# First-unit inputs in one queue, the mask spread by a product, both first units ahead of the scores: a cross-attention and feed-forward kernel on one core

## The chip, the core and the metric

The kernel runs on one core of a Trainium2 chip. The metric is device time in microseconds (us) of one execution; lower is better. Three timed runs of the kernel before gave 1829.25, 1832.85 and 1832.66 us, median 1832.66. One more execution was profiled, and all durations below come from it. In its views the engines are PE (TensorE matmuls; PEld its weight loads), DVE (VectorE), ACT (ScalarE), POOL (GpSimd) and SP (SyncE, which here only issues DMAs). SPq, ACTq and POOLq are the instruction streams that issue DMAs.

## The reference

Sixteen sequences, each with 256 rows (channels) of 512 positions, float32:

```python
x = x + xattn(layernorm(x), ctx, mask, mask, Wq, bq, Wk, bk, Wv, bv)   # 16 heads of 16 channels
x = x + ffn(layernorm(x), lut, gate_idx, up_idx, down_idx)             # weights are lut[idx], 1376 wide

# xattn: q = Wq @ target + bq, k and v likewise from source; per head
dot = mask * (q.T @ k) / 4 - (1 - mask) * 1e6
out = (softmax(dot) * mask) @ v
```

The layernorm runs over the 512 positions of a row, without weights. The mask is one row of 512 numbers per sequence, used for queries and for keys.

## The kernel before

All of it is float32. The attention part takes the first 1000 us or so, the feed-forward part the rest. This case concerns the first 50 us.

**Units and steps.** Heads are handled four at a time. A *unit* is four heads of one sequence, and there are 64 units. Each head owns a strip of 32 partitions in the tiles `kp` (keys) and `qp` (queries): 16 rows of data and two rows that carry the mask term and the row maximum, so that one 32-row product gives masked scores less their maximum. Each unit has four *steps*, one per 128 query positions. A step makes scores twice. First `pa` (L483) gives the scores that DVE reduces to row maxima (`nm`, L499). Seven steps later `pb` (L491) gives the transposed scores, which ACT turns into exponentials (L503) for the product with the values (L525). Steps are numbered by their `pb`, so steps -7 to -1 have `pa` only, and step 0 is the first with both. The maxima of a unit are turned (`turn_max`, tile `pmx`), copied by DVE and sent by a POOL DMA into `qp`.

**The order is written out by hand.** `scores(sa, sb)` makes the score products of a step. The dictionary `lumps[s]` holds PE work put after the scores of step `s` and `after[s]` what follows it: projections of later units (`project(k, "k")`, `project(k, "q")`), values (`project_v`), sends through DRAM (`send`, `fetch`), statistics (`stats1`), the layernorm of the next sequence (`norm1`, on POOL), and so on. Every engine then runs its own list strictly in this order, and an instruction that has to wait holds up all behind it on that engine. The PSUM pool `ps_a` has two buffers of two banks (the two halves of a `pa`); `ps_b` has four of one bank, shared by everything else on PE.

**Ahead of step -7** come the first units, 0 and 1 (`e` = 0 and 1 of the first eight heads). They do not go through DRAM. `pad(i, e)` copies the wanted columns of `wk` or `wq` into strips of a zeroed tile `w0`; `first_tile(which, e)` multiplies them with the source `cx0` or the normalized rows `xn0`, adds a per-row column `bcol` and multiplies with a mask tile (`mbk` for keys, `mb0` for queries). `bcol` is a transpose (tile `pbrow`) of the small tile `brow`, into which four POOL DMAs bring biases. `mbk` is the mask row broadcast to 128 partitions by a DMA, two rows of each strip then being overwritten by two more DMAs (L376, L377): the mask less one, computed by DVE at L375 from `mk16`, and ones. `mb0` is the plain broadcast. `row_stats` (L100, L101), `rstd1_of` (ACT's square root at L105, then L106 and L107) and `norm1` (L282) normalize `xn0`. `warm(n)` issues n transposes of the identity that nothing reads. Unit 0 is made ahead of step -7; unit 1's `pad` and `first_tile` stand in steps -7 to -4.

**DMA counters.** A DMA that SP or ACT issues signals its landing on one of eight counters, taken in turn. A DMA that takes a counter again first waits, on its own issuing engine, until the counter's earlier DMA has landed.

Of the kernel before, what the change touches and what calls it, by code (L numbers as in the profile page):

```python
# [9 lines left out]
F32 = mybir.dt.float32  # L10
I32 = mybir.dt.int32
AF = mybir.ActivationFunctionType
ALU = mybir.AluOpType
# [6 lines left out]
def kernel(  # L20
# [70 lines left out]
    lut_b = cpool.tile([P, LUT], F32, tag="lut", name="lut_b")  # L91
# [6 lines left out]
    def row_stats(pool, mv, xt, name):  # L98
        st = pool.tile([P, 6], F32, tag="bn", name=f"bn_{name}")
        nc.vector.bn_stats(st, xt)  # L100
        nc.vector.bn_aggr(mv, st)  # L101
# [117 lines left out]
    with ExitStack() as att:  # L219
        ac = att.enter_context(tc.tile_pool(name="att_const", bufs=1))  # L220
        p1 = att.enter_context(tc.tile_pool(name="att1", bufs=1))
        p2 = att.enter_context(tc.tile_pool(name="att2", bufs=2))
        pp = att.enter_context(tc.tile_pool(name="att_p", bufs=3))
        lp = att.enter_context(tc.tile_pool(name="lookup", bufs=1))

        wq = ac.tile([P, NCC, C], F32, tag="wq", name="wq")
# [22 lines left out]
        def times(row, n):  # L249
            return row.rearrange("p (o t) -> p o t", o=1).to_broadcast([1, n, T])  # L250
# [27 lines left out]
        def norm1(b, eng):  # L278
            xn = inp[b][1]
            for o in range(NCC):  # L280
                i = b * NCC + o
                eng.tensor_scalar(  # L282
                    xn[:, o, :], xn[:, o, :], rstd1[:, i : i + 1], nmr1[:, i : i + 1],
                    ALU.mult, ALU.add,
                )

        def set_ones(i):
            nc.gpsimd.memset(vas[i][:, :, :, D : 2 * D], 1.0)
# [3 lines left out]
        xn0 = p2.tile([P, NCC, T], F32, tag="xn", name="xn_0")  # L292
        mb0 = p2.tile([P, T], F32, tag="mb", name="mb_0")
        inp[0] = (cx0, xn0, mb0)
        for o in range(NCC):
            nc.sync.dma_start(xn0[:, o, :], x[0, o * P : (o + 1) * P, :])
        nc.scalar.dma_start(wk, wkT.rearrange("(o p) n -> p o n", p=P))
        nc.scalar.dma_start(cx0, src[0].rearrange("(o p) t -> p o t", p=P))
        nc.sync.dma_start(mk16, mask[:, 0, :])
        nc.sync.dma_start(mb0, mask[0, 0].partition_broadcast(P))  # L300

        w0 = pp.tile([P, 4, NCC, P], F32, tag="pt", name="w0")
        nc.gpsimd.memset(w0, 0.0)
        nc.gpsimd.memset(ones, 1.0)


        brow = pp.tile([P, P], F32, tag="pt", name="brow")
        nc.vector.memset(brow, 0.0)
        nc.vector.memset(brow[0:64, 16:P:32], NEG / QK)
        for i in range(2):  # L310
            nc.vector.memset(brow[64:P, 16 + i : P : 32], 1.0)

        mbk = pp.tile([P, T], F32, tag="pt", name="mbk")
        nc.sync.dma_start(mbk, mask[0, 0].partition_broadcast(P))
        nc.sync.dma_start(wq, wqT.rearrange("(o p) n -> p o n", p=P))
        for i, w in enumerate((bq, bk)):
            for e in range(2):
                at = 64 * i + 32 * e
                nc.gpsimd.dma_start(
                    brow[at : at + 1].rearrange("o (j e d) -> o j e d", e=2, d=D)[:, :, 0],  # L320
                    w[0:P].rearrange("(o j e d) -> o j e d", o=1, e=2, d=D)[:, :, e],
                )
        n = B * NCH
# [5 lines left out]
        nc.scalar.dma_start(wv, wvT.rearrange("(o p) n -> p o n", p=P))  # L329
        nc.scalar.dma_start(bvb, bv.partition_broadcast(P))  # L330
        nc.scalar.dma_start(lut_b, lut.partition_broadcast(P))
        zeros = rpool.tile([P, T], F32, tag="rb", name="zeros", bufs=1)
        nc.gpsimd.memset(zeros, 0.0)

# [13 lines left out]
        def pad(i, e):  # L348
            w = (wk, wq)[i]
            to = w0[:, 2 * i + e].rearrange("p o (j r) -> p o j r", r=32)[:, :, :, 0:16]  # L350
            of = w[:, :, 0:P].rearrange("p o (j e d) -> p o j e d", e=2, d=D)[:, :, :, e]
            if i == 0:
                nc.vector.tensor_copy(to, of)
            else:
                nc.vector.tensor_scalar(to, of, QK, None, ALU.mult)

        def first_tile(which, e):

            i, to, m = (0, kps[e], mbk) if which == "k" else (1, qps[e], mb0)
            ps = ps_b.tile([P, 512], F32, tag="b", name=f"p{which}_first{e}")  # L360
            for o in range(NCC):
                nc.tensor.matmul(
                    ps, w0[:, 2 * i + e, o, :], inp[0][i][:, o, :],
                    start=(o == 0), stop=(o == NCC - 1),
                )
            at = 64 * (1 - i) + 32 * e
            nc.vector.scalar_tensor_tensor(to, ps, bcol[:, at : at + 1], m, ALU.add, ALU.mult)

        def warm(n):
            for _ in range(n):  # L370
                ps = ps_b.tile([P, 512], F32, tag="b", name="warm")
                nc.tensor.transpose(ps[:, :P], ident, ident)

        warm(60)
        nc.vector.tensor_scalar(mk16, mk16, -1.0, None, ALU.add)  # L375
        nc.sync.dma_start(mbk[16:P:32, :], times(mk16[0:1], 4))  # L376
        nc.sync.dma_start(mbk[17:P:32, :], ones[0:4])  # L377
        for o in range(NCC):
            row_stats(p2, mv1[:, o, :], xn0[:, o, :], f"a0_{o}")
        pad(0, 0)  # L380
        rstd1_of(0, 1)
        norm1(0, nc.vector)
        pad(1, 0)
        pc = ps_b.tile([P, 512], F32, tag="b", name="pbrow")
        nc.tensor.transpose(pc[:, :P], brow, ident)
        bcol = pp.tile([P, P], F32, tag="pt", name="bcol")
        nc.vector.tensor_copy(bcol[:, 64:P], pc[:, 64:P])
        nc.vector.tensor_scalar(bcol[:, 0:64], pc[:, 0:64], QK, None, ALU.mult)
        first_tile("k", 0)
        first_tile("q", 0)  # L390
# [23 lines left out]
        def project(k, which):  # L414
            b, oc = divmod(k, NCC)
            cx, xn, mb = inp[b]
            w, src_t = (wk, cx) if which == "k" else (wq, xn)
            ps = ps_b.tile([P, 512], F32, tag="b", name=f"p{which}_{k}")
            in_columns(ps, lambda o, at: w[:, o, at], oc * P, lambda o: src_t[:, o, :])
            t = p1.tile([P, T], F32, tag=f"nat{which}", name=f"nat{which}_{k}")  # L420
            if which == "k":
                nc.scalar.activation(t, ps, AF.Identity, bias=bkc[:, oc : oc + 1])  # L422
            else:
                nc.scalar.activation(t, ps, AF.Identity, bias=bqc[:, oc : oc + 1], scale=QK)
            nc.gpsimd.tensor_tensor(t, t, mb, ALU.mult)  # L425
            nat[which, k] = t
# [14 lines left out]
        def project_v(k, i):  # L441

            b, half = divmod(k, 2)
            cx = inp[b][0]
            c = 2 * half + i
            ps = ps_b.tile([P, 512], F32, tag="b", name=f"pv_{b}_{c}")
            in_columns(ps[:, :C], lambda o, at: cx[:, o, at], c * P, lambda o: wv[:, o, :])
            vt = p2.tile([P, C], F32, tag="vt", name=f"vt_{b}_{c}")
            nc.scalar.copy(vt, ps[:, :C])
            nc.gpsimd.tensor_tensor(  # L450
                vas[b % 2][:, c, :, 0:D], vt.rearrange("p (h d) -> p h d", d=D),
                bvb.rearrange("p (h d) -> p h d", d=D), ALU.add,
            )
# [148 lines left out]
        for k in range(1, NK):  # L602
            t = 8 * k
# [593 lines left out]
```

## Time and profile before

| | |
|---|---|
| median of the timed runs (3) | 1832.66 us (1829.25 to 1832.85) |
| profiled execution, its own time | 1828.26 us |
| its span, first to last instruction | 1826.5 us |
| PE busy over the span | 1800.2 us (99%) |
| DVE busy | 1453.9 us (80%) |
| ACT busy | 800.8 us (44%) |
| PE busy from 0 to 14 us, 14 to 20 us, 20 to 50 us | 12.01, 4.15, 27.41 us |
| start of step -7 (first `pa`), of step 0, of step 2 | 16.67, 40.94, 49.79 us |

The timeline view lists merged instructions with start, duration, engine, line, operation, output, input and count; a square bracket gives the idle time of the engine before it and what ended that. The windows view gives, for stretches of the span, each engine's busy time and instruction count, the clock granted to TensorE (1.00 is full) and what the DMA engines moved. The waits view gives who waited for whom: total us, times, longest.

### The profile page before, as it was taken

Reading aid. Unit: us, or ns where it says so; the run is one execution under the profiler, and the core shown is the slowest. Engines: PE = TensorE matmul, PEld = TensorE weight load, DVE = VectorE, ACT = ScalarE, POOL = GpSimd, SP = SyncE. Lnnn points to the kernel's source line nnn. Section 1 sums busy time; section 2 is a strip of 40 time slices with the busy share of each in tenths; the row PEclk is TensorE's granted clock in tenths of the full one; section 3 lists DMA queues with packets and bytes.
Section 4 is the critical chain, followed back from the end, with each engine's and each line's share of the span. In section 5 each row is a group of like instructions: output and inputs, shape, how many; then the busy total and the mean of one; then the engine's idle time right before and its main releaser. Section 6 shows DMA issues by size and latency. Waiting matters only on the chain.

```text
span 1826.5 us, 28462 instructions
## 1 busy us (share of the span) xinstructions
PE 1800.2 (99%) x10914; PEld 811.5 (44%) x10914; DVE 1453.9 (80%) x1979; ACT 800.8 (44%) x1523; POOL 499.1 (27%) x465
## 2 busy tenths in 40 slices
PE   8999999999999999999999999999999999999999
PEld 4333333333333333333343444444444444588888
DVE  6898999999999999999874699998989964354352
ACT  1777677777777777777777111112121111000000
POOL 4334333434343434343322122222222222000000
PEclk9999999999999999999999999999999999999999
DMA  6545244334443444445242211223121311533531
GB/s 188 152 140 157 90 128 119 118 96 119 130 120 93 116 136 123 128 126 149 91 128 83 75 51 63 75 86 104 64 98 53 110 46 42 183 131 120 182 131 58
DMA packets 118535, 201.07 MB, mean 110 GB/s; under 512 B 21748, under 2 KB 23416, under 8 KB 118400
## 3 DMA queue, kind: packets, MB, share of 16 engines
q1 hardware_dynamic: 114128, 196.21, 34.4%
q0 software_dynamic: 3168, 1.86, 0.5%
q8 instruction: 86, 1.41, 0.3%
q10 hardware_dynamic: 1104, 1.19, 0.2%
q14 instruction: 49, 0.40, 0.1%
HBM read 135.83 MB, written 58.10 MB: 106 GB/s over the span
## 4 chain that ended last, share of the span: by engine, by line
PE 83%; DMA 6%; DVE 5%; issue 2%; SPq 2%; POOL 2%; ACT 0%; POOLq 0%; DVEq 0%; ACTq 0%
PE p L894 27%; PE pa L483 13%; PE q L1100 11%; PE pv L525 10%; PE pb L491 9%; PE pk L409 3%; PE pv L409 3%; PE pq L409 2%; DVE nm L499 2%; PE po L1081 2%; DMA qp<-qd 2%; PE q L1105 1%; PE pgu L874 1%; PE pmx L508 1%; PE pt L215 1%
## 5 line engine op out<-in xcount | busy, mean ns | idle before, releaser
L499 DVE TENSOR_REDUCE nm<-pa 128x2 f32<-128x1024 f32 x512 | 602.0, 1217 | 75.6 <-PE pb L491 70.1
L503 ACT ACTIVATE pt<-pb 128x512 f32<-128x512 f32 x1024 | 531.3, 603 | 114.2 <-PE pb L491 112.5
L483 PE MATMUL pa<-kp,qp 32*128 32x512 f32 x2048 | 520.7, 618 | 12.3 <-DVE nm L499 7.4
L491 PE MATMUL pb<-qp,kp 32*128 32x512 f32 x2048 | 518.8, 619 | 0.0
L483 PEld LDWEIGHTS pa<-kp,qp 32*128 32x128 f32 x2048 | 181.1, 184 | 226.2 <-DVE nm L499 190.4
L525 PE MATMUL pv<-pt,va 128*32 128x512 f32 x2048 | 246.5, 599 | 0.0
L491 PEld LDWEIGHTS pb<-qp,kp 32*128 32x128 f32 x2048 | 201.1, 183 | 74.7 <-issue 46.7
L894 PE MATMUL p<-xe,wu 128*128 128x512 f32 (+1 forms) x336 | 158.1, 593 | 1.0 <-DVE w L898 1.0
L894 PE MATMUL p<-xT,sw 128*128 128x512 f32 (+1 forms) x336 | 157.9, 592 | 0.0
L894 PE MATMUL p<-xT,wg 128*128 128x512 f32 (+1 forms) x336 | 157.9, 592 | 0.0
L921 POOL TENSOR_TENSOR ha<-ha,sg 128x512 f32<-128x512 f32 (+1 forms) x42 | 59.8, 1424 | 345.0 <-DVE ha L898 333.9
L926 ACT ACTIVATE w<-w 128x512 f32<-128x512 f32 (+1 forms) x42 | 26.5, 630 | 239.9 <-DVE w L898 239.9
L525 PEld LDWEIGHTS pv<-pt,va 128*32 128x32 f32 x2048 | 53.4, 109 | 174.1 <-ACT pt L503 97.8
L511 POOL DMA_DIRECT2D qp<-mx x64 | 37.5, 585 | 314.6 <-DVE mx L510 213.1
L1116 ACT COPY q<-q 128x256 f32<-128x256 f32 x14 | 5.2, 372 | 254.1 <-PE q L1100 254.1
L530 ACT COPY us<-pv 128x512 f32<-128x512 f32 x128 | 74.9, 585 | 93.0 <-PE pv L525 92.3
L894 PEld LDWEIGHTS p<-xe,wu 128*128 128x128 f32 (+1 forms) x336 | 62.8, 187 | 83.0 <-issue 72.0
L894 PEld LDWEIGHTS p<-xT,wg 128*128 128x128 f32 (+1 forms) x336 | 62.7, 187 | 79.2 <-issue 76.4
L894 PEld LDWEIGHTS p<-xT,sw 128*128 128x128 f32 (+1 forms) x336 | 62.1, 187 | 75.4 <-issue 73.4
L908 ACT ACTIVATE sg<-sg 128x512 f32<-128x512 f32 (+1 forms) x42 | 26.5, 630 | 154.7 <-DVE sg L898 154.7
L537 POOL TENSOR_TENSOR us<-us,us 128x512 f32<-128x512 f32 x64 | 82.2, 1285 | 16.5 <-ACT us L530 16.4
L425 POOL TENSOR_TENSOR natk<-natk,mb 128x512 f32<-128x512 f32 x31 | 42.8, 1381 | 158.0 <-ACT natk L422 152.4
(182 smaller groups left out, 2373.3 us busy)
## 6 DMA issues: line engine op xcount, KB each, us to landing
x2t<-x SPq DMA_DIRECT2D x96, 256.0 KB
h<-h SPq DMA_DIRECT2D x7, 2560.0 KB
kp<-kd SPq DMA_DIRECT2D x62, 256.0 KB
qp<-qd SPq DMA_DIRECT2D x62, 256.0 KB
h<-ha SPq DMA_DIRECT2D x38, 256.0 KB
h<-hb SPq DMA_DIRECT2D x38, 256.0 KB
rb<-rd SPq DMA_DIRECT2D x32, 256.0 KB
xr<-in_x_dram SPq DMA_DIRECT2D x32, 256.0 KB
```

The lines of the kernel that those rows point to most:

```text
L409: nc.tensor.matmul(ps[32 * j : 32 * j + 32], weights(o, slice(first + 32 * j, first + 32 * j + 32)), moving(o), start=(o == 0), stop=(o == ...
L425: nc.gpsimd.tensor_tensor(t, t, mb, ALU.mult)
L483: nc.tensor.matmul(pa[:, jj, :], qps[ua % 4][at, ca * P : (ca + 1) * P], kps[ua % 4][at, :], start=True, stop=True,)
L491: nc.tensor.matmul(pb, kps[ub % 4][at, cb * P : (cb + 1) * P], qps[ub % 4][at, :], start=True, stop=True,)
L499: nc.vector.tensor_reduce(nms[ua][:, 2 * half : 2 * half + 2, ca], pa, AX.X, ALU.max, negate=True)
L503: nc.scalar.activation(pts[sb][:, j, :], pb, AF.Exp)
L525: nc.tensor.matmul(ps[32 * j : 32 * j + 32, :], va[:, at : at + 32], pt[:, j, :], start=(i == 0), stop=(i == 1),)
L530: nc.scalar.copy(us[u, half], ps)
L537: nc.gpsimd.tensor_tensor(a, a, b, ALU.add)
L894: nc.tensor.matmul(ps, a[:, h, at], b[:, h, :], start=h == 0, stop=h == 1)
L921: nc.gpsimd.tensor_tensor(ha, ha, sg, ALU.mult)
L1100: nc.tensor.matmul(ps, a[:, o, first_t], b[:, o, :], start=o == 0, stop=o == HO - 1 and not more,)
```

## The change

It touches only what stands ahead of step 0.

- **Loads.** `xn0`, `wk`, `cx0`, `wq`, `mk16`, `wv`, `bvb`, `lut_b` are all issued by SP, in this order. The four bias DMAs into `brow` move from POOL to ACT. The three broadcasts and the two patches that made `mbk` and `mb0` are gone.
- **Mask.** Two rows of a zeroed tile `msrc` are loaded with the mask by two ACT DMAs, DVE subtracts one from the second, and two matmuls with a selection tile `sel` (built by DVE memsets) write `mbk` and `mb0` into one PSUM tile `pm`. ACT copies them out.
- **Order.** `warm(60)` becomes `warm(24)` and, after the mask and `bcol`, `warm(12)`. The statistics of `xn0` now follow `bcol`. All four `pad` come next (those with `e` = 1 on ACT) and then all four `first_tile`, ahead of step -7.
- **Steps -7 to 0.** The four lumps that made unit 1 fall away. `project_v` of the first sequence moves from steps -3 to -1 to steps -5 and -4; `project(2, "k")` and `project(2, "q")` move one step earlier, to -2 and -1; `set_ones(1)` moves from step -4 to -6.

```diff
-        nc.scalar.dma_start(wk, wkT.rearrange("(o p) n -> p o n", p=P))
-        nc.scalar.dma_start(cx0, src[0].rearrange("(o p) t -> p o t", p=P))
-        nc.sync.dma_start(mk16, mask[:, 0, :])
-        nc.sync.dma_start(mb0, mask[0, 0].partition_broadcast(P))
...
+        msrc = xpool.tile([P, T], F32, tag="xT", name="msrc")
+        sel = xpool.tile([P, 2, P], F32, tag="xT", name="sel")
+        nc.gpsimd.memset(msrc, 0.0)
...
-        nc.sync.dma_start(mbk, mask[0, 0].partition_broadcast(P))
-        nc.sync.dma_start(wq, wqT.rearrange("(o p) n -> p o n", p=P))
+        for o in range(NCC):
+            nc.sync.dma_start(xn0[:, o, :], x[0, o * P : (o + 1) * P, :])
         for i, w in enumerate((bq, bk)):
             for e in range(2):
                 at = 64 * i + 32 * e
-                nc.gpsimd.dma_start(
+                nc.scalar.dma_start(
...
+        nc.sync.dma_start(wk, wkT.rearrange("(o p) n -> p o n", p=P))
+        for i in range(2):
+            nc.scalar.dma_start(msrc[32 * i : 32 * i + 1], mask[0, 0:1, :])
+        nc.sync.dma_start(cx0, src[0].rearrange("(o p) t -> p o t", p=P))
+        nc.sync.dma_start(wq, wqT.rearrange("(o p) n -> p o n", p=P))
+        nc.sync.dma_start(mk16, mask[:, 0, :])
+        nc.vector.memset(msrc[64:65], 1.0)
+        nc.vector.memset(sel, 0.0)
...
+            for o in range(NCC):
+                if e:
+                    nc.scalar.activation(to[:, o], of[:, o], AF.Copy, scale=QK if i else 1.0)
...
-        warm(60)
-        nc.vector.tensor_scalar(mk16, mk16, -1.0, None, ALU.add)
-        nc.sync.dma_start(mbk[16:P:32, :], times(mk16[0:1], 4))
-        nc.sync.dma_start(mbk[17:P:32, :], ones[0:4])
-        for o in range(NCC):
-            row_stats(p2, mv1[:, o, :], xn0[:, o, :], f"a0_{o}")
-        pad(0, 0)
-        rstd1_of(0, 1)
-        norm1(0, nc.vector)
-        pad(1, 0)
+        warm(24)
+        nc.vector.tensor_scalar(msrc[32:33], msrc[32:33], -1.0, None, ALU.add)
+        pm = ps_a.tile([P, 2, 512], F32, tag="a", name="pm")
+        for i, to in enumerate((mbk, mb0)):
+            nc.tensor.matmul(pm[:, i, :], sel[0:96, i, :], msrc[0:96], start=True, stop=True)
+            nc.scalar.copy(to, pm[:, i, :])
         pc = ps_b.tile([P, 512], F32, tag="b", name="pbrow")
         nc.tensor.transpose(pc[:, :P], brow, ident)
...
-        first_tile("k", 0)
-        first_tile("q", 0)
+        warm(12)
+        for o in range(NCC):
+            row_stats(p2, mv1[:, o, :], xn0[:, o, :], f"a0_{o}")
+        rstd1_of(0, 1)
+        norm1(0, nc.vector)
+        pad(0, 0)
+        pad(0, 1)
+        pad(1, 0)
+        pad(1, 1)
+        for e in range(2):
+            first_tile("k", e)
+            first_tile("q", e)
+        nc.vector.tensor_scalar(mk16, mk16, -1.0, None, ALU.add)
...
-        after[-7].append(lambda: (pad(0, 1), pad(1, 1)))
-        lumps[-5].append(lambda: first_tile("k", 1))
-        lumps[-4].append(lambda: first_tile("q", 1))
...
-        lumps[-1].append(lambda: project(2, "k"))
-        lumps[0].append(lambda: project(2, "q"))
+        lumps[-2].append(lambda: project(2, "k"))
+        lumps[-1].append(lambda: project(2, "q"))
...
-        lumps[-3].append(lambda: project_v(0, 0))
-        lumps[-2] += [lambda: project_v(0, 1), lambda: project_v(1, 0)]
-        lumps[-1].append(lambda: project_v(1, 1))
+        lumps[-5] += [lambda: project_v(0, 0), lambda: project_v(0, 1)]
+        lumps[-4] += [lambda: project_v(1, 0), lambda: project_v(1, 1)]
...
-        after[-4].append(lambda: set_ones(1))
+        after[-6].append(lambda: set_ones(1))
```

More of the change, by code (lines that the diff above doesn't have):

```diff
@@ L294 @@
         inp[0] = (cx0, xn0, mb0)
-        for o in range(NCC):
-            nc.sync.dma_start(xn0[:, o, :], x[0, o * P : (o + 1) * P, :])
-        nc.scalar.dma_start(wk, wkT.rearrange("(o p) n -> p o n", p=P))
-        nc.scalar.dma_start(cx0, src[0].rearrange("(o p) t -> p o t", p=P))
-        nc.sync.dma_start(mk16, mask[:, 0, :])
-        nc.sync.dma_start(mb0, mask[0, 0].partition_broadcast(P))
-        w0 = pp.tile([P, 4, NCC, P], F32, tag="pt", name="w0")
-        nc.gpsimd.memset(w0, 0.0)
-        nc.gpsimd.memset(ones, 1.0)
+        msrc = xpool.tile([P, T], F32, tag="xT", name="msrc")
+        sel = xpool.tile([P, 2, P], F32, tag="xT", name="sel")
         brow = pp.tile([P, P], F32, tag="pt", name="brow")
+        nc.gpsimd.memset(msrc, 0.0)
         nc.vector.memset(brow, 0.0)
@@ L311 @@
             nc.vector.memset(brow[64:P, 16 + i : P : 32], 1.0)
-        mbk = pp.tile([P, T], F32, tag="pt", name="mbk")
-        nc.sync.dma_start(mbk, mask[0, 0].partition_broadcast(P))
-        nc.sync.dma_start(wq, wqT.rearrange("(o p) n -> p o n", p=P))
+        for o in range(NCC):
+            nc.sync.dma_start(xn0[:, o, :], x[0, o * P : (o + 1) * P, :])
         for i, w in enumerate((bq, bk)):
@@ L322 @@
                 )
+        nc.sync.dma_start(wk, wkT.rearrange("(o p) n -> p o n", p=P))
[6 more added lines that the diff above has]
+        nc.vector.memset(sel, 0.0)
+        nc.vector.memset(sel[0:1], 1.0)
+        for i in range(2):
+            nc.vector.memset(sel[0:1, 0, 16 + i : P : 32], 0.0)
+            nc.vector.memset(sel[32 + 32 * i : 33 + 32 * i, 0, 16 + i : P : 32], 1.0)
+        w0 = pp.tile([P, 4, NCC, P], F32, tag="pt", name="w0")
+        nc.gpsimd.memset(w0, 0.0)
+        nc.gpsimd.memset(ones, 1.0)
+        mbk = pp.tile([P, T], F32, tag="pt", name="mbk")
         n = B * NCH
@@ L328 @@
         nc.gpsimd.dma_start(mq16, mask[:, 0, :])
-        nc.scalar.dma_start(wv, wvT.rearrange("(o p) n -> p o n", p=P))
-        nc.scalar.dma_start(bvb, bv.partition_broadcast(P))
-        nc.scalar.dma_start(lut_b, lut.partition_broadcast(P))
+        nc.sync.dma_start(wv, wvT.rearrange("(o p) n -> p o n", p=P))
+        nc.sync.dma_start(bvb, bv.partition_broadcast(P))
+        nc.sync.dma_start(lut_b, lut.partition_broadcast(P))
         zeros = rpool.tile([P, T], F32, tag="rb", name="zeros", bufs=1)
@@ L351, in pad @@
             of = w[:, :, 0:P].rearrange("p o (j e d) -> p o j e d", e=2, d=D)[:, :, :, e]
-            if i == 0:
+            for o in range(NCC):
+                if e:
+                    nc.scalar.activation(to[:, o], of[:, o], AF.Copy, scale=QK if i else 1.0)
+            if not e and i == 0:
                 nc.vector.tensor_copy(to, of)
-            else:
+            elif not e:
                 nc.vector.tensor_scalar(to, of, QK, None, ALU.mult)
@@ L372, in warm @@
                 nc.tensor.transpose(ps[:, :P], ident, ident)
-        warm(60)
-        nc.vector.tensor_scalar(mk16, mk16, -1.0, None, ALU.add)
-        nc.sync.dma_start(mbk[16:P:32, :], times(mk16[0:1], 4))
-        nc.sync.dma_start(mbk[17:P:32, :], ones[0:4])
-        for o in range(NCC):
-            row_stats(p2, mv1[:, o, :], xn0[:, o, :], f"a0_{o}")
-        pad(0, 0)
-        rstd1_of(0, 1)
-        norm1(0, nc.vector)
-        pad(1, 0)
+        warm(24)
[4 more added lines that the diff above has]
+            nc.scalar.copy(to, pm[:, i, :])
         pc = ps_b.tile([P, 512], F32, tag="b", name="pbrow")
```

## The prediction

> **What bounds the kernel now.** The page comes first: PE is busy 99% of the span, so what counts is when PE is held up, and the change can move the end only by the holds of the first 50 us. The timeline of that stretch shows them:
>
> ```profile
> 6.92 0.38 SPq L315 DMA_DIRECT2D wq<-in_L_xattn_Wq_dram  x1
> 7.21 0.69 DVE L100 BATCH_NORM_STATS2 bn_a<-xn 128x6 f32<-128x512 f32 x1
> 8.95 0.29 ACT L105 ACTIVATE rstd<-mv,eps 128x2 f32<-128x2 f32 x1 [2.87 <-DVE mv L101]
> 9.67 1.00 DVE L282 TENSOR_SCALAR xn<-xn,rstd,nmr 128x512 f32<-128x512 f32 x2
> 11.09 1.96 PE L362 MATMUL pk_first<-ctx,w 128*128 128x512 f32 x4
> 11.39 0.55 SPq L377 DMA_DIRECT2D mbk<-mrows  x1
> 15.21 0.75 DVE L367 SCALAR_TENSOR_TENSOR kp<-pk_first,bcol,mbk 128x512 f32<-128x512 f32 x1 [2.90 <-DMA mbk<-mrows]
> 16.67 1.14 PE L483 MATMUL pa<-kp,qp 32*128 32x512 f32 x8 [1.85 <-DVE qp L367]
> 42.82 2.07 ACT L503 ACTIVATE pt<-pb 128x512 f32<-128x512 f32 x4
> 43.52 1.92 PE L409 MATMUL pq<-xn,wq 128*32 128x512 f32 x16 [0.57 <-POOL va L450]
> 49.79 0.69 PE L483 MATMUL pa<-kp,qp 32*128 32x512 f32 x1
> ```
>
> Step -7 starts at 16.67, step 2 at 49.79, and from 50 to 60 us the windows show PE busy all 10.00 us. So I count the start of step 2: a shift there goes to the end unless a later hold takes it up. Next the waits view of 0 to 45 us:
>
> ```profile
> DVE mrows L375 <- DMA mrows<-in_mask_Bx1x_fk_dram: 5.5, 1, 5.5
> DVE kp L367 <- DMA mbk<-mrows: 2.9, 1, 2.9
> PE pa L483 <- DVE qp L367: 2.7, 2, 1.8
> ```
>
> The mask patches hold PE 1.85 us ahead of step -7; that is nearly all the change can win there. Last the windows (columns: stretch, length, busy PE, PEld, DVE, ACT, POOL with counts, granted clock, DMA share, GB/s):
>
> ```profile
> 1.40:2.40 1.00, 1.00 (x5) 1.00 (x6) 0.00 (x0) 0.00 (x0) 0.94 (x2) 1.00 0.57 68
> 2.40:3.40 1.00, 1.00 (x7) 1.00 (x6) 0.00 (x0) 0.00 (x0) 1.00 (x2) 1.00 0.94 337
> 3.40:4.40 1.00, 1.00 (x6) 1.00 (x5) 0.00 (x0) 0.00 (x0) 1.00 (x3) 1.00 1.08 400
> 4.40:5.40 1.00, 1.00 (x6) 1.00 (x6) 0.00 (x0) 0.61 (x1) 1.00 (x3) 1.00 0.99 356
> 5.40:6.40 1.00, 1.00 (x9) 1.00 (x8) 0.00 (x0) 0.68 (x1) 1.00 (x3) 1.00 1.05 388
> 6.40:7.40 1.00, 1.00 (x11) 1.00 (x10) 0.61 (x2) 0.00 (x0) 0.96 (x3) 1.00 1.02 339
> 183.00:186.00 3.00, 1.41 (x21) 0.47 (x18) 2.49 (x5) 1.65 (x4) 0.00 (x0) 1.00 0.40 126
> 188.00:190.00 2.00, 2.00 (x12) 0.34 (x12) 1.97 (x3) 1.33 (x3) 1.98 (x3) 0.50 0.19 47
> ```
>
> Two readings. Transposes run at 6 per us until about 5.4 us and at 11 after: PE starts slow and speeds up with work, though the clock column says 1.00. And after a stretch with 1.41 us of work in 3.00 the granted clock falls to 0.50.
>
> **The front, step by step.** What decides is the order on DVE, ACT and PE after the change. DVE's statistics stand behind the copies of `bcol`, those behind PE's `pbrow`, that behind both mask products, and these behind the second row of `msrc`, which DVE must lower by one. Before, the statistics started at 7.21 on nothing but `xn0`. And the second row's DMA takes the counter that `wq`'s load uses, so ACT issues it only when `wq` has landed.
>
> *When `wq` lands.* SP's queue must move `xn0`, `wk`, `cx0` and `wq`: 256+256+256+512+256 KB = 1.54 MB. The windows from 1.40 to 6.40 sum to 68+337+400+356+388 = 1.55 MB whatever queue issued them. So 6.4, with the signal 6.6.
>
> *When the row lands, T.* No row shows a 2 KB ACT load. Nearest rows: the patch at L377, issued 11.39, let DVE go at about 15.1 (3.7); the first 256 KB of `xn0`, issued 0.74, released SP at 3.74 (3.0); `mk16`, behind 512 KB, 5.1 (1.65 to 6.74). From 6.65 that gives 9.0 with some of the 3.0 off for its own data, 10.0 midway between the first two, 11.7 at worst. I take **T = 10.0**. The Trainium skill, "DMA: Bandwidth & Descriptors", section "Anatomy of one DMA", puts the fixed cost of a DMA, on POOL's path, at about 2.0 us; by it T would be 8.7 and everything after 1.3 earlier.
>
> *From T to the first tile.*
> - L387 on DVE as L375: 0.42, to 10.4.
> - One mask product is half of a first tile's 1.96: 0.98 at the fast rate, about 1.9 at the slow one. The 24 warming transposes end near 5.4, when the rate had just changed, and PE then has nothing for 5 us; the row at 183 us lost the clock on less. I take 1.9, to 12.35. ACT's copy as `us` (0.59): 12.95. The second product waits for that copy: 14.85; `pbrow` 0.30 to 0.55: 15.3.
> - `bcol` 0.22+0.21: 15.8. Statistics 7.21 to 8.91 = 1.70: 17.5. ACT's square root to the end of `norm1`, 8.95 to 10.67 = 1.72: 19.25. ACT's extra table loads (1.28 each) lie under T and under the statistics. `pad` 0.21: 19.45. `pad` on ACT and the load of `wq` are long done.
> - Four first tiles at 1.93 = 7.72: 27.2, at the fast rate. Ahead of them PE has done the products and 12 transposes and then idles 2.5 to 3 us. If that drops the clock for one stretch of 3.4 us as after 186 us, half of it, 1.7, is lost; I take 1.0: **28.2**.
>
> Dropped at no cost or gain: 36 warming transposes (PE idles there anyway), broadcasts (256 KB twice), the bias DMAs on ACT (some 0.5 us each, all ahead of 6.6), DVE's memsets (under 2 us, over before T).
>
> Which clock rule holds moves these terms. The Trainium skill, "TensorE: Matmul & The Clock Gate", Part 1, says that a free-running window of about 3.4 us sets the rate and an idle one drops it to half; Part 4 adds that transposes don't count as work. The rows agree with the first (0.50 after 183) and speak against the second (6 per us becomes 11 on transposes alone). By the second, all four first tiles would begin slow: 1.7 in place of my 1.0.
>
> **Steps -7 to 2.** Counted from the end t of the fourth first tile; PE rows: a `pa` pair 1.06, projection 1.85, two value projections 1.9, DVE reduction 1.18.
> - Step -7: `pcols`, `pa`, `pk` end at t+3.3. DVE has L379 (0.75), L409 (0.42), L413 and L414 (0.39) and L415 (0.41) before its first reduction at t+2.0, so the second half of the next `pa` waits to t+4.4: step -5 starts at t+7.3.
> - Steps -5 and -4 with two value projections each are PE's: t+13.8. Step -3 has only `pmx` (0.3) over DVE's 2.36: step -2 at t+16.1, its second half at t+17.3, `pk` done t+20.2.
> - DVE's statistics for the next sequence end at t+21.6, square root and L107 at t+22.4, POOL's `norm1` halves at t+23.2 and t+23.9. `project(2, "q")`, now ahead of step 0, needs them: done t+25.1 in place of t+23.2. Before, the same `norm1` was hidden.
> - Step 0 follows. On ACT, strictly in order: `natq` 0.69, the table load 1.28, four exponentials 2.07, `mask_v` 1.69, four more 2.07 = 7.8 us, to t+32.9. `pb` has four buffers and `pmx` and a value projection want them too, so step 2 starts at **t+33.0**. Before, the table load lay beside step 0 (41.52).
>
> The same arithmetic on the old order, from 16.67, gives 49.35 for the real 49.79, so I add 0.2: step 2 at 28.2+33.2 = 61.4 against 49.79: **+11.6 us**.
>
> Bounds: T 9.0 and the fast rate throughout give 9.0+0.45+0.98+0.62+0.98+0.3+0.5+1.7+1.75+0.2+7.7 = 24.2, step 2 at 57.2, +7.4. T 11.7, slow products and a full 1.7 give 30.6, step 2 at 64.0, +14.2.
>
> **What a later hold can give back.** PE's idle time from 50 to 1000 us is 10.5 us (windows), and the half clock after 186.8 lost 1.7. The largest place is 182 to 192: 2.1 idle and that 1.7, behind a load of `xs`. SP issues this load in the same order behind the same sends, so I give back nothing and keep 3.8 as its bound.
>
> On the profiled execution's own 1828.26 that is 1839.9 (1835.7 to 1842.5). It lies 4.4 under the median of the timed runs; on the median the sum is 1844.3 (1840.1 to 1846.9). The forecast sits between: **1842 us**.
>
> **Rivals.**
> 1. *A short wait* (0.20): the row lands as T 9.0 and PE stays fast. +7.4: 1835.7 to 1840. For: nothing else is on ACT's queue. Against: DMA share near 1.0 at 6.4.
> 2. *Slow clock and late row* (0.12): +14.2 or a little over: 1842.5 to 1849. For: the row at 183 us.
> 3. *The hold at 182 to 192 dissolves over a short front* (0.09): 7.4-3.8 = 3.6, to 1832 to 1836: no change. For: 1832.85 beside 1829.25 says some executions already differ by 3.6 us.
> 4. *Faster* (0.05): attention runs later against SP's prefetches, and the waits of `pa` between 50 and 1000 us, 10.5+1.7 = 12.2 us, are given back. Price at best 7.4-12.2 = -4.8: 1823.5 to 1828. It decides once over 7.4 us return. Against: SP waits for `natk` and `natq` of each unit, so its lead does not grow.
>
> The forecast itself has 0.54. Without rivals a front that gains is excluded: step 2 before 49.79 needs t under 16.6, a first tile at 8.9, ahead of T.
>
> **Numbers.** A measurement tells 0.2% (3.7 us) from no change: 1829.0 to 1836.3 is the same. Faster 0.05; same 0.09 and a quarter of rival 1, 0.14; slower 0.81. Range 1832 to 1849: from rival 3's lower end to rival 2's upper one.
>
> **What would show it.** Right: L387 starts near 10, behind `wq`; `bn_a` of the first sequence after 15; first `pk_first` near 19.5; first `pa` near 28.6; `pq` of unit pair 2 waits for POOL's `xn`; step 2 near 61. Wrong: L387 before 8, `pk_first` before 15, or step 2 later by over 10 with the end less than 5 later, which would mean a later hold took it up.

## The result, and the profile after

The changed kernel is slower: 1847.65 us median of four runs (1847.03 to 1851.40) against 1832.04 for the kernel before beside it, ratio 1.0094, 95% interval 1.008 to 1.0108. On the 1832.66 that the forecast started from, that is 1849.9: 7.9 above the forecast and 0.9 above the end of its range. A second comparison gave 1.0086 (1.0072 to 1.0101). The sign and the mechanism were as forecast; the size was not.

The profiled execution took 1847.81 us, its span is 1846.0. Its timeline, with the columns as before:

```profile
2.90 1.19 ACTq L311 DMA_DIRECT2D brow<-in_L_xattn_bk_dram  x2
...
3.44 0.37 SPq L319 DMA_DIRECT2D wq<-in_L_xattn_Wq_dram  x1
...
8.31 0.56 ACTq L317 DMA_DIRECT2D msrc<-in_mask_Bx1x_fk_dram  x2
...
13.73 0.42 DVE L387 TENSOR_SCALAR msrc<-msrc 1x512 f32<-1x512 f32 x1 [10.13 <-DMA msrc<-in_mask_Bx1x_fk_dram]
...
14.25 2.05 PE L390 MATMUL pm<-msrc,sel 96*128 96x512 f32 x2 [7.90 <-DVE msrc L387]
...
16.97 2.07 PE L390 MATMUL pm<-msrc,sel 96*128 96x512 f32 x2 [0.68 <-ACT mbk L391]
...
19.30 0.23 DVE L395 COPY bcol<-pbrow 128x64 f32<-128x64 f32 x1 [5.15 <-PE pbrow L393]
...
19.68 0.69 DVE L100 BATCH_NORM_STATS2 bn_a<-xn 128x6 f32<-128x512 f32 x1
...
22.15 1.00 DVE L282 TENSOR_SCALAR xn<-xn,rstd,nmr 128x512 f32<-128x512 f32 x2
...
23.39 3.39 PE L374 MATMUL pk_first<-ctx,w 128*128 128x512 f32 x4 [1.58 <-issue]
...
31.92 1.14 PE L502 MATMUL pa<-kp,qp 32*128 32x512 f32 x8
...
50.43 3.47 PE L428 MATMUL pk<-ctx,wk 128*32 128x512 f32 x16
...
57.01 3.59 PE L428 MATMUL pq<-xn,wq 128*32 128x512 f32 x16 [2.04 <-POOL xn L282]
...
68.34 0.69 PE L502 MATMUL pa<-kp,qp 32*128 32x512 f32 x1
```

The reader sees the forecast's chain link by link: the mask rows are issued only at 8.31, DVE gets the second at 13.73, the products follow, then `bcol`, then the statistics, which stood at 7.21 before and now stand at 19.68. The first `pa` comes at 31.92 in place of 16.67, step 2 at 68.34 in place of 49.79: 18.55 us later, and the span is 19.5 longer. The waits view names the same links:

```profile
DVE msrc L387 <- DMA msrc<-in_mask_Bx1x_fk_dram: 10.1, 1, 10.1
PE pm L390 <- DVE msrc L387: 7.9, 1, 7.9
PE pq L428 <- POOL xn L282: 2.0, 1, 2.0
PE pk_first L374 <- issue: 1.6, 1, 1.6
```

The windows view (stretch, length, busy PE, PEld, DVE, ACT, POOL, granted clock, DMA share, GB/s) shows what the forecast had too small:

```profile
4.40:5.40 1.00, 1.00 (x6) 1.00 (x6) 0.00 (x0) 0.00 (x0) 1.00 (x3) 1.00 0.75 208
9.00:13.00 4.00, 0.00 (x0) 0.00 (x0) 0.00 (x0) 1.18 (x1) 1.15 (x2) 0.53 0.93 220
14.00:20.00 6.00, 5.08 (x10) 2.29 (x11) 0.82 (x4) 1.49 (x3) 0.00 (x0) 0.50 0.82 315
50.00:54.00 4.00, 4.00 (x22) 0.76 (x24) 3.31 (x6) 0.02 (x1) 0.33 (x1) 0.57 0.30 102
54.00:57.00 3.00, 0.97 (x8) 0.14 (x8) 2.08 (x3) 0.85 (x2) 2.06 (x3) 1.00 0.54 169
57.00:60.00 3.00, 2.99 (x16) 0.59 (x16) 1.42 (x3) 0.00 (x0) 0.70 (x1) 0.50 0.43 142
```

From 9 to 13 us PE does nothing, the DMA engines are 93% busy, and the clock falls to half. The clock is low from 9.2 to 26.3, and in two more stretches, 50.2 to 53.6 and 57.0 to 60.4, in which `pk` takes 3.47 and `pq` 3.59 us, where the same products take 1.92 at the full clock (e14 below).

### The profile page after: what moved, and what is told of

It is laid out like the page before. It is cut to its first block, busy times and chain, and to the rows that moved or that the text cites. A ratio compares the mean times of both kernels' runs of the same rounds, so it can differ in the third digit from the quotient of the medians.

```text
span 1846.0 us, 28431 instructions
## 1 busy us (share of the span) xinstructions
PE 1809.5 (98%) x10894; PEld 813.3 (44%) x10894; DVE 1455.5 (79%) x1985; ACT 803.6 (44%) x1530; POOL 496.6 (27%) x462
## 4 chain that ended last, share of the span: by engine, by line
PE 79%; DMA 7%; DVE 5%; SPq 2%; issue 2%; POOL 2%; ACT 1%; POOLq 0%; ACTq 0%; DVEq 0%
PE p L909 26%; PE pa L502 12%; PE q L1115 9%; PE pv L544 9%; PE pb L510 9%; PE pv L428 3%; PE pk L428 2%; PE pq L428 2%; DVE nm L518 2%; PE po L1096 2%; DMA x2t<-x 2%; DMA qp<-qd 1%; DMA xr<-in_x_dram 1%; PE pgu L889 1%; PE q L1120 1%
```

## The experiments

Three numbers of each trace carry most of what the experiments told: when the first `pa` starts (the front), how long it is from there to step 2 (the steps), and how many stretches at half clock, of 3.4 us each, lie between.

| kernel | first `pa` | half-clock stretches | first `pa` to step 2 | step 2 | ratio to before (95%) |
|---|---|---|---|---|---|
| before | 16.67 | 0 | 33.12 | 49.79 | 1 |
| changed | 31.92 | 2 | 36.42 | 68.34 | 1.0094 (1.008, 1.0108) |
| changed, again (e14) | 31.62 | 0 | 33.09 | 64.71 | 1.0086 (1.0072, 1.0101) |
| rows first (e1) | 22.14 | 2 | 36.40 | 58.54 | 1.0034 (1.0021, 1.0047) |
| more warming (e2) | 28.39 | 2 | 36.37 | 64.76 | 1.0075 (1.0058, 1.0092) |
| old steps (e3) | 32.40 | 2 | 34.31 | 66.71 | 1.0088 (1.0073, 1.0103) |
| statistics first (e4) | 29.30 | 1 | 34.73 | 64.03 | 1.0082 (1.0067, 1.0097) |
| rows and statistics first (e5) | 15.86 | 0 | 33.09 | 48.95 | 1.0 (0.999, 1.0009) |
| the same, unit 0 alone (e6) | 14.27 | 0 | 33.11 | 47.38 | 0.9981 (0.9971, 0.9991) |
| before, new order alone (e7) | 18.58 | 1 | 34.39 | 52.97 | 1.0003 (0.9992, 1.0015) |
| e5 with idle transposes (e8) | 16.39 | 0 | 34.25 | 50.64 | 0.9994 (0.9982, 1.0006) |
| changed with idle transposes (e9) | 34.06 | 0 | 34.26 | 68.32 | 1.0088 (1.0064, 1.0111) |
| before, mask by product alone (e11) | 16.69 | 0 | 33.12 | 49.81 | 0.9992 (0.9982, 1.0002) |
| e6 with PE interleaved (e12) | 17.02 | 0 | 33.12 | 50.14 | 0.9987 (0.9975, 0.9999) |
| DVE zeroes `msrc` (e13) | 26.87 | 2 | 36.41 | 63.28 | 1.0054 (1.0036, 1.0073) |
| e9 again (e15) | 31.06 | 0 | 34.25 | 65.31 | 1.0084 (1.0071, 1.0097) |

**Is the row the head of the chain (e1)?** The two row DMAs go first on ACT, so DVE, not POOL, zeroes the tile:

```diff
-        nc.gpsimd.memset(msrc, 0.0)
+        nc.vector.memset(msrc[0:96], 0.0)
+        for i in range(2):
+            nc.scalar.dma_start(msrc[32 * i : 32 * i + 1], mask[0, 0:1, :])
         # (the same two lines further down are taken out)
```

> One edit to the changed kernel: the two mask-row DMAs of msrc are issued by ACT ahead of the four bias DMAs (the zeroing of msrc is done by DVE instead of POOL so that they need not wait for POOL), so neither row waits for the landing of wq or of a bias. Theory A (the front is set by when the second mask row lands, 13.70 us in the changed kernel): L387 starts at 4 to 6 us, pm follows at 5 to 7, the first pk_first starts between 12.5 and 14.5 instead of 23.4, step 2 at 57 to 60 instead of 68.3, and the time falls by 8 to 11 us. Rival B (something else, such as the late loads of wk, cx0 or wq, sets the front): pk_first does not start before 20 us and the time falls by less than 3 us.

```profile
1.47 0.77 ACTq L307 DMA_DIRECT2D msrc<-in_mask_Bx1x_fk_dram  x2
...
4.76 0.42 DVE L387 TENSOR_SCALAR msrc<-msrc 1x512 f32<-1x512 f32 x1 [1.24 <-DMA msrc<-in_mask_Bx1x_fk_dram]
...
13.52 3.48 PE L374 MATMUL pk_first<-ctx,w 128*128 128x512 f32 x4 [2.69 <-issue]
```

In the timeline L387 moves from 13.73 to 4.76, and the first `pa` and step 2 move with it by 9.8. The end follows: 1.0094 becomes 1.0034. So the row is the head.

**What makes the row late: the counter or the data ahead of it (e13)?** Only the memset moves; the rows stay behind the biases in ACT's list. With POOL's memset the first row's DMA takes the counter of the last bias DMA and the second that of `wq`; with DVE's, both take counters of `xn0`.

```diff
-        nc.gpsimd.memset(msrc, 0.0)
+        nc.vector.memset(msrc[0:96], 0.0)
```

> The changed kernel with one line changed: msrc is zeroed by DVE (rows 0 to 95) instead of POOL. The rows of msrc stay behind the biases in ACT's list, but their DMAs then take the counters of the two xn0 loads and no longer wait for wq and the last bias. Theory (the term T of the forecast was late by a gate of 1.9 us and by a landing under full queues of 1.8 us more than assumed): the rows are issued near 4.2 instead of 8.3 to 9.4, land under load in 4 to 5 us, and L387 starts between 8.2 and 9.5 instead of 13.5 to 15.6; step 2 moves by as much less the bias landings, 3.5 to 5.5 us, and the end with it. Rival (the row waits for the data queued ahead of it, not for its counter): L387 at 12 or later, step 2 moves by less than 2.

```profile
4.71 0.74 ACTq L317 DMA_DIRECT2D msrc<-in_mask_Bx1x_fk_dram  x2
...
8.62 0.42 DVE L387 TENSOR_SCALAR msrc<-msrc 1x512 f32<-1x512 f32 x1 [5.11 <-DMA msrc<-in_mask_Bx1x_fk_dram]
...
18.26 3.47 PE L374 MATMUL pk_first<-ctx,w 128*128 128x512 f32 x4 [1.57 <-issue]
```

In e14, the changed kernel on the same chip, the two lines are:

```profile
8.78 0.54 ACTq L317 DMA_DIRECT2D msrc<-in_mask_Bx1x_fk_dram  x2
...
14.87 0.42 DVE L387 TENSOR_SCALAR msrc<-msrc 1x512 f32<-1x512 f32 x1 [11.28 <-DMA msrc<-in_mask_Bx1x_fk_dram]
```

The rows are issued at 4.71 in place of 8.78, and DVE starts at 8.62 in place of 14.87. Of these 6.25 us, 4.1 are the earlier issue and 2.2 a shorter flight, 3.9 in place of 6.1. The counter's wait is the larger part. The first `pa` is 4.75 earlier, as the theory asked; step 2 only 1.4, because this execution had two half-clock stretches and e14 none. The medians on this chip are 1841.91 and 1845.66. The landings of the counters agree: in all seven traces with POOL's memset the first row is issued 0.08 to 0.09 us after the last bias has landed (8.23 and 8.31 in the first).

**Does the slow clock in front cost, and do transposes hold it (e2)?**

```diff
-        warm(24)
+        warm(96)
...
-        warm(12)
+        warm(40)
```

> One edit to the changed kernel: warm(24) becomes warm(96) and warm(12) becomes warm(40), transposes that nothing reads, so that PE has work until the mask row lands and until pad is done. Theory C (PE at half rate from 9.1 to 26.2 us costs what the products took beyond the fast rate): pm takes about 1.0 us each instead of 2.05, the first pk_first 1.9 to 2.0 instead of 3.4, L387 still at 13.5 to 14, the fourth first tile ends 3.5 to 4.5 us earlier (27.5 to 28.5 instead of 31.9) and the time falls by 3 to 5 us if the clock drops at 50 and 57 us stay as they are; if they go or grow, by up to 7 or down to 0. Rival D (transposes do not count as work for the clock, as the page on TensorE says): the granted clock still falls near 9 us, pm stays at 2 us, and the time stays within 1 us.

The row came at 13.52, as before. The windows view shows a full clock on transposes alone, and the products and first tiles run at the fast rate:

```profile
9.00:13.00 4.00, 4.00 (x39) 4.00 (x38) 0.00 (x0) 1.28 (x1) 1.15 (x2) 1.00 0.81 178
```
```profile
14.04 1.10 PE L390 MATMUL pm<-msrc,sel 96*128 96x512 f32 x2
...
21.37 1.88 PE L374 MATMUL pk_first<-ctx,w 128*128 128x512 f32 x4
```

The first `pa` is at 28.39 in place of 31.92: the slow clock in front cost 3.3 us once 0.2 of earlier row is taken off. So transposes are work for the clock here, and the time in which PE had none was paid for afterwards at the low clock.

**Do the statistics belong behind `bcol` (e4)?** `row_stats`, `rstd1_of`, `norm1` and the four `pad` move ahead of L387.

> One edit to the changed kernel: row_stats, the square root, norm1 and the four pads stand ahead of L387 on DVE and ACT, as the mask row does not concern them. Theory G (PE's own chain of mask product, copy, mask product, pbrow and 12 transposes ends at 21.8 and is next in line): the statistics start near 4 us, the first pk_first starts at 21 to 22 instead of 23.4, 1.5 to 2.3 us are won, a little more if PE's clock comes back earlier. Rival H (the order on DVE is what costs most): pk_first starts before 19 us and over 4 us are won.

The row was as late as ever (13.50), yet the first `pa` came at 29.30, 2.6 earlier (0.2 of it by the row). The chain from statistics to `norm1` had been on the path. It was not worth the 3.5 us of its own length (19.68 to 23.15), because `pk_first` then stood right behind the second `warm` (18.82 to 21.59 at the slow clock): it started at 21.38 in place of 23.39 and took 2.78 in place of 3.39.

**What do the steps cost (e3, e7)?** e3 puts the lumps of the changed kernel back to their old steps, without unit 1's tiles. e7 is the kernel before with the new order alone (`pad` and `first_tile` of both units ahead, the same moves in the lumps).

> The changed kernel's front with the steps -7 to 0 of the kernel before, but for unit 1's tiles, which stay ahead of the scores: project_v back in steps -3 to -1, project(2, k) in -1, project(2, q) in 0, set_ones(1) after -4. Theory E (the new places of the projections cost 1.5 us in waits on DVE, POOL and ACT, and bring the two half-rate stretches at 50.2 and 57.0 us): step 2 starts 31.5 us after the fourth first tile plus what the clock loses, against 36.4 measured, so the time falls by 2 to 5 us. Rival F (the new places are neutral, the clock drops come from the DVE-bound steps in any order): within 1.5 us of the changed kernel, with as many half-rate stretches.

> The kernel before with the third part of the change alone: both units' pads and tiles ahead of step -7, the values, project(2) and set_ones moved as in the changed kernel; loads and mask as before. Theory (the order itself costs because PE is given less to do in steps -3 to -1 and project(2, q) waits for norm1 of the next sequence): fourth tile ends near 18.7, step 2 near 51.9 (+2.1) if the clock holds and near 55 (+5) with two stretches at half rate; the end +2 to +5. Rival (the order is neutral, all of the loss sits ahead of step -7): step 2 between 49.5 and 50.5, the end within 1 us of before.

e3 saves 2.1 us between the first `pa` and step 2, with two half-clock stretches in both (in e3 back to back, from 43.9 to 50.8). So the new places of the projections cost some 2 us next to the old places without unit 1's tiles, if two stretches cost the same in both. Its end (1.0088) can't be told from the changed kernel's. e7 moves step 2 by 3.2: 1.9 is the later first `pa`, 1.3 the steps, which had one half-clock stretch. Its end, -1.5 to +2.7 us, says no more than that the order alone is a small part of the loss.

**Is the half clock in steps -2 and -1 the change's fault (e9, e14, e15, e8)?** Idle transposes are put where PE waits:

```diff
+        lumps[-3].append(lambda: warm(10))
-        lumps[-2].append(lambda: project(2, "k"))
-        lumps[-1].append(lambda: project(2, "q"))
+        lumps[-2] += [lambda: project(2, "k"), lambda: warm(8)]
+        lumps[-1] += [lambda: warm(18), lambda: project(2, "q")]
```

> The changed kernel with idle transposes where PE waits: 10 in step -3, 8 in step -2 behind project(2, k), 18 in step -1 ahead of project(2, q); the front is untouched. The changed kernel had two stretches at half rate there (50.2 to 53.6 and 57.0 to 60.4), and its step 2 stood 36.4 us behind the fourth first tile, against 33.2 in the kernel with the quick front, which had none. Theory (those two stretches cost 3.2 us and come from PE's idle time ahead of them): no stretch at half rate between 40 and 65 us, the fourth first tile ends near 32 as before, step 2 near 65.5 to 66.5 (the transposes themselves cost up to 1.7, as in the quick-front pair), the end 2 to 3 us earlier than the changed kernel's. Rival (steps -2 to 1 are bound by DVE and ACT whatever the clock): step 2 at 68 or later, 36 us behind the fourth tile.

> The changed kernel once more, on the chip of these comparisons, as the base for the run with idle transposes and the run with DVE's memset, and to see how much the landing of the row differs between executions (L387 between 13.5 and 15.6 in the five executions with this front so far). Theory: two stretches at half rate between 45 and 62 us again, step 2 36 us behind the fourth first tile. Rival (the drops are chance): none or one stretch there.

> The changed kernel with idle transposes in steps -3 to -1 once more, beside the changed kernel on the same chip. Theory (the half clock there costs 2 to 3 us): fourth first tile to step 2 in 34.4 against 36.4 us, and the median 1.5 to 3 us under the changed kernel's. Rival (what the clock loses there is given back at a later hold, or lost in the spread of the row's landing): medians within 1 us of each other.

> The kernel with the front of e5_front and the order of the changed kernel, with idle transposes added where PE waits: 10 in step -3, 8 in step -2 behind project(2, k), 18 in step -1 ahead of project(2, q). Theory (the half clock in steps -2 and -1 costs 3.2 us and comes from PE's idle time there): no stretch at half rate between 20 and 50 us, step 2 3 us earlier than in e5_front, near 50.3, the end 3 us earlier than e5_front's. Rival (the clock drops for another reason, or steps -2 to 1 are bound by DVE and ACT anyway): step 2 as in e5_front or later.

With the transposes there was no stretch there in any of three traces, and the steps took 34.25. (The base of e8, e5, turned out to have none either, so e8's step 2 came 1.7 us later than e5's, not earlier.) But the changed kernel itself, run again (e14), had none either:

```profile
50.04 1.92 PE L428 MATMUL pk<-ctx,wk 128*32 128x512 f32 x16
...
55.06 1.92 PE L428 MATMUL pq<-xn,wq 128*32 128x512 f32 x16 [2.03 <-POOL xn L282]
...
64.71 0.69 PE L502 MATMUL pa<-kp,qp 32*128 32x512 f32 x1
```

The same program took 36.42 with two stretches and 33.09 with none. The table puts a price on them: 0, 1 and 2 stretches give 33.09, 34.39 to 34.73, and 36.37 to 36.42, 1.3 to 1.7 us each. Whether they come differs from execution to execution. With the transposes the steps are 1.16 us longer than at a full clock without them, and the medians, 1846.80 with and 1845.66 without them on one chip, show no gain. The theory that this clock is a fixed cost of the change has fallen. It is a risk that came with it: of the eight traces with the new steps and no transposes six had one or two stretches, of the four with the old steps (before, e6, e11, e12) none. In e9 moreover the row came 1.9 us later than in the first trace and hid what was won.

The traces also show a pattern in when they come. All changes of the clock in a trace lie on one grid of 3.41 us, which stands differently against the kernel in each execution. From the first `pa` to the next line of this grid it is 1.1 to 1.3 us in the four traces with two stretches (changed, e1, e2, e13), 0.7 and 2.7 in the two with one (e4, e7), and 2.3 in the two with none (e5, e14). e8, e9 and e15, with transposes, lie at 0.5, 1.5 and 1.3 and had none. No run set the grid on purpose, so this is a pattern and not a test.

**What are the parts worth once the row is early (e5, e6, e11, e12)?** e5 has the rows first, then `row_stats`, L387, `rstd1_of`, `norm1` and two `pad` on DVE, no second `warm`. e6 is e5 with unit 0 alone in front and the old steps. e11 is the kernel before with rows first and the mask by a product in place of the two broadcasts and two patches, nothing else. e12 is e6 with PE's order mask product, `pbrow`, `pk_first`, mask product, `pq_first`.

> Two edits of the front together: the rows of msrc are issued first on ACT, and the statistics, the square root, norm1 and the pads stand around the mask's subtraction instead of behind bcol; the second warm goes. The rows-first run had its first tile at 13.52 and the statistics-first run had everything of DVE done early. Theory (the front is a chain of order: row, products, bcol, statistics): both gains add, the first pk_first starts at 9.4 to 9.7, four tiles end near 17.1, step 2 near 50.3 if the clock holds in steps -3 to 0 and near 53.5 if two stretches at half rate come there as in all runs so far. The end is then +0.5 to +4 us from the kernel before. Rival (the queue of the loads decides, the order on DVE little): the first tile cannot start before 12, step 2 at 56 or later, the end +6 or more.

> The front of the run before (rows first, statistics ahead), with the order of the kernel before behind it: unit 0 alone ahead of step -7, unit 1's pads, tiles, the values and project(2) back in the steps where they stood. The mask is still spread by a product and the loads are in one queue. Theory (parts one and two of the change are worth something once the row is early, part three costs): the first pa at 14.1 against 16.67 before, step 2 near 47.2 against 49.79, the end 2.6 us before the kernel before, ratio 0.9986. Rival (what PE gains in front is lost to a clock at half rate or a wait in steps -7 to 0): step 2 at 49.8 or later, the end equal or later than before.

> The kernel before with the second part of the change alone: the mask rows are loaded first on ACT and spread by two products, no broadcasts and no patches; the loads stay in their three queues, the biases on POOL, unit 0 alone ahead of step -7, all steps as before. Theory (the mask patches hold step -7 by 1.85 us, and behind them stands pbrow, whose biases come on POOL near 10.9): the first pk_first stays at 11.1, first pa near 15.6 against 16.67, step 2 near 48.7 (-1.1), the end 1 us earlier. Rival 1 (the patches were the only hold): first pa at 14.8 or earlier, step 2 near 47.9. Rival 2 (the products are only worth it with the loads in one queue): step 2 at 49.8 or later.

> The kernel with the quick front and unit 0 alone, with PE's order in front changed: mask product for the keys, pbrow, pk_first, mask product for the queries, pq_first, so that PE does pk_first while ACT copies, and the pad that waits for wq stands behind the copies of bcol. Theory (0.68 us of PE idle time between the products and 0.5 behind them are filled): first pa near 13.4 against 14.27, step 2 near 46.6 against 47.38, the end 0.8 us earlier, which the times can hardly tell from the kernel with the old order. Rival (pq_first waits for wq's landing or the rest of the front for DVE): first pa at 14.1 or later.

e5 does all that the change wants and is as fast as the kernel before:

```profile
8.84 1.88 PE L374 MATMUL pk_first<-ctx,w 128*128 128x512 f32 x4
...
15.86 1.14 PE L501 MATMUL pa<-kp,qp 32*128 32x512 f32 x8
```

e6 beats both: first `pa` at 14.27 and step 2 at 47.38, as expected to 0.2, and the end 1.7 to 5.3 us earlier than before. Its `pk_first` starts at 9.71:

```profile
9.71 1.94 PE L374 MATMUL pk_first<-ctx,w 128*128 128x512 f32 x4
...
14.27 1.14 PE L498 MATMUL pa<-kp,qp 32*128 32x512 f32 x8 [0.84 <-DVE qp L379]
```

e11 missed: the mask was there at 4.64, but the front did not move. In its timeline the products stand behind 60 warming transposes and ahead of `pbrow`:

```profile
1.37 8.22 PE L381 MATMUL warm<-ident 128*128 128x128 f32 x60 [1.37 <-POOL ident masks.py:199]
...
9.42 1.02 PE L393 MATMUL pm<-msrc,sel 96*128 96x512 f32 x2
...
11.12 1.13 PE L393 MATMUL pm<-msrc,sel 96*128 96x512 f32 x2 [0.68 <-ACT mbk L394]
...
12.08 0.28 PE L396 MATMUL pbrow<-ident,brow 128*128 128x128 f32 x1
...
12.20 1.88 PE L371 MATMUL pk_first<-ctx,w 128*128 128x512 f32 x4
```

`pk_first` moves from 11.09 to 12.20, and the wait for the patches (1.85) has become work and waits on PE. So the product alone is worth nothing. A shorter `warm` with it was not tried; by an estimate from the two starts of `pk_first` (12.20 and 11.09) it could win 1.1 us, because in the kernel before `pbrow` itself waited for the last bias (which comes by POOL there, as in e11):

```profile
10.94 0.30 PE L385 MATMUL pbrow<-ident,brow 128*128 128x128 f32 x1 [0.63 <-DMA brow<-in_L_xattn_bk_dram]
```

e12 missed on the other side: 17.02 in place of the 13.4 expected. `pbrow`, moved ahead of `pk_first`, waited for the last bias:

```profile
9.77 0.30 PE L406 MATMUL pbrow<-ident,brow 128*128 128x128 f32 x1 [2.69 <-DMA brow<-in_L_xattn_bk_dram]
...
9.90 2.67 PE L376 MATMUL pk_first<-ctx,w 128*128 128x512 f32 x4
```

The clock was at half from 11.0 to 14.4, which took in the second half of `pk_first` and the second product (1.91):

```profile
11.00:14.00 3.00, 3.00 (x4) 1.03 (x4) 0.75 (x1) 0.00 (x0) 0.00 (x0) 0.50 0.94 242
```

In e6 PE had that product to do meanwhile, `pbrow` came at 9.57 and the clock held. e12's first `pa` is later in the trace by 2.8; the two ratios, 0.9987 and 0.9981, don't tell them apart.

## Why the prediction was right, and where it was wrong

**The yardstick held.** A shift of step 2 goes to the end: +18.55 became +19.5 in the span, and in all sixteen profiled executions it is 1775.2 to 1780.9 us from step 2 to the end of the span (1776.7 before, 1777.7 after). So a shift goes through, to within some 4 us in one execution. Nothing is given back at the hold of 182 to 192 us either: it moves along with the kernel. Behind it, step 41 starts at 218.58 in place of 200.14, still 18.44 later, and step 233 at 937.36 in place of 919.41, 17.95 later. PE's idle time from 60 to 1000 us is 11.7 us after and 10.5 before. Rivals 3 and 4 fall. Rival 1, the short wait, falls with L387 at 13.50 or later in all seven traces of this front.

**"When `wq` lands", 6.6, and T = 10.0: the step that failed.** Two terms were too small, by 3.7 us together: the gate opened at 8.31 in place of 6.65, and from there it took 5.42 us in place of 3.35 until DVE went on.

The gate: the landings on the counters have the last bias at 8.23 and `wq` at 8.54. The sum had `wq` land once 1.55 MB had moved; by 8.40 the windows sum to 1.95 MB. Other loads were moving beside it, `wv` (issued at 4.50) and POOL's among them, and it went slower in between: 208 GB/s from 4.40 to 5.40 where 356 stood; why was not tested. The bias DMAs were in the sum only as 0.5 us of issue each, "all ahead of 6.6"; that the first row shares a counter with the last of them was not in it. In the first trace this cost next to nothing, as the second row waited for `wq` anyway; in four of the other six the bias landed after `wq`.

The flight: from the first row's issue to L387 it took 4.2 to 6.2 us in the seven traces with this front, L387 at 13.50 to 15.60. The rows it was taken from, a patch at 11.39 and the very first load, flew while the DMA engines were 72% and 63% busy; here it was 94% from 8.30 to 14.00. e1 and e11, issued at 1.5, took 3.2 to 3.3; e13, at 4.71, 3.9. The busy share alone does not sort them (e1 had 83%, e2, with 4.2 us, 81%), so what lengthens the flight stays open. The Trainium skill, "DMA: Bandwidth & Descriptors", section "Anatomy of one DMA", has about 2.0 us as a constant cost on POOL's path; these rows went by ACT, and none was as quick.

**T to the first tile was right.** Forecast 9.45, measured 23.39 - 13.73 = 9.66: products 2.05 for 1.9, statistics 1.7, square root to `norm1` 1.72.

**Four tiles with 1.0 of lost clock**: 8.72 forecast, 8.53 measured, 7.09 in e14, where the clock was back at 23.6. Inside that allowance.

**Steps -7 to 2**: 32.8 from the first `pa`, measured 33.09 wherever the clock held. `pq` waits for POOL's `xn` as said. With the clock low it is 36.4, and that was not in the sum: I had let the clock fall in front only. In front, the transposes that were dropped "at no cost" did cost: e2 wins 3.3 us with more of them, of which the sum had 2.8 under other names (0.9 for each slow product, 1.0 for the tiles).

So step 2 missed 61.4 by 6.9 in the first trace: the first `pa` 3.3 late (3.7 from T, 0.4 back from the tiles and behind them), the steps 3.6 too long (3.3 from the clock, 0.3 in the sum). In e14 it missed by 3.3: the first `pa` 3.0 late (4.9 from T, 1.9 back), the steps 0.3. T is the miss that both share. Rival 2, slow clock and late row, was nearest (64.0); its T of 11.7 was too low as an upper bound. (By their own terms the two bounds of step 2 are 24.2 + 33.2 = 57.4 and 30.6 + 33.2 = 63.8, not 57.2 and 64.0.)

**What the change cost, by runs.** Of the 15.25 us by which the first `pa` is later, taking the row first gives back 9.8 (e1), and putting the statistics ahead of `bcol` and dropping the second `warm` another 6.3 (e5), which ends 0.8 ahead of before; unit 1's two tiles in front cost 1.6 (e6 to e5) to 1.9 (before to e7). The new steps are as long as the old ones while the clock holds, 33.09 against 33.12, although unit 1's two tiles are out of them. By e3 the old places would have been some 2 us shorter without these tiles, so the new places use up what the tiles leave free; the old places without the tiles were not seen at a full clock. What the single queue is worth by itself was not tried; e6 and e12, the two versions whose interval lies below 1, have it together with the early row, the product, the early statistics and the shorter `warm`.

## What to carry to other kernels

Before moving a small load, ask which counter or slot it will take and what has to land first: here one memset on another engine moved a 2 KB load by 4 us. Put work that depends on nothing new (the statistics) ahead of the wait that is being added, not behind it, and price a wait of PE with the clock that it loses. A product that replaces a transfer has its own place in PE's list; put behind 60 transposes, as in e11, it won nothing.

## What the runs showed of the hardware

- Transposes alone kept the clock full: 1.00 from 9 to 13 us with 39 float32 transposes and nothing else on PE (e2), and 0.53 with none (changed kernel). The Trainium skill, "TensorE: Matmul & The Clock Gate", Part 4, says that they don't count as busy in the same way as other work; here they kept the clock up.
- Half-clock stretches are 3.41 us or a multiple long in all traces (but for the last one, at the end of the kernel), and one program had two between its first `pa` and step 2 in one execution and none in another. Part 1 of the same page has a free-running window of about 3.4 us; the traces agree. On this path a stretch cost 1.3 to 1.7 us.
- By the landings on the counters, the second 2 KB row took 2.6 to 2.7 us from issue to landing when issued at 2.0 us (e1, e11), and 3.8 to 5.9 us when issued at 8.6 to 10.2 (the seven traces with POOL's memset), where the DMA engines were 81 to 99% busy from 9 to 13 us.
